# Chunked attention on one core: the off-diagonal weight blocks replaced by folded states

## Chip, core and metric

The kernel runs on one core of a Trainium2 chip, in one launch. The metric is the device time of that launch in microseconds (us). Everything is float32.

## What is computed

The input `x` has 8 sequences of 256 tokens with 256 features. One layer is computed: `x + attention(layernorm(x)) + ffn(layernorm(x))`. The change touches only the second half of the attention, for 16 heads with key and value size 128 and 64 memory slots (M = 64):

```
q, k = rope(hs @ Wq.T), rope(hs @ Wk.T);  v = hs @ Wv.T
s    = clip(hs @ Ws1.T @ Ws2.T + bs2);  es = exp(s);  enz = exp(-cumlogsumexp(s))
A    = causal(q @ k.T) * scale
ok   = enz * (A @ es)                 # T x M
qv   = softmax(ok)                    # T x M
W2   = causal((qv * enz) @ es.T)      # T x T
o    = W2 @ v                         # T x 128
out  = (rmsnorm(o) * silu(g)) @ Wo.T
```

A sequence of 256 tokens is two chunks of 128. In `W2` there are three blocks of 128 by 128 that aren't zero: two on the diagonal, which are triangular, and one below it, which is full: second chunk's queries against first chunk's keys.

## The kernel before

Tokens are taken in four groups of 512 (two sequences each, `TC` = 4 chunks of 128), heads in pairs. One step `n` is one group and one pair of heads, so there are 32 steps. A step's stages are functions: `rope` (q and k), `value` and `gate` (both through `vg`), `states` (es, es transposed, enz), `scores`, `logits`, `softmax`, `turn` (the softmax transposed and multiplied by enz: `prT`), `weights`, `outputs`, `turn_back`, and every second step `close` (the product with Wo). The feed-forward part (`ffn_block`, `ffn_down`) is fed in between these stages.

The order of the work is written out by hand. Each stage has a place in its step, a fraction in the table `POS` at the top of the file; the loop at the end of `layer_kernel` sorts the stages of a step by it and calls them. A stage issues its TensorE work at once and leaves the work of the other engines behind as a generator in `chains`; each call of `tick()` moves every such generator on by one piece. `need(...)` ticks until the given generators are through, and so only sets the order in which instructions are issued; the waits on the chip are semaphores. Step `n` runs the front of step `n` (scores, logits, softmax), the first stages of `n + 1` (states, rope) and the back of `n - 1` (turn, weights, outputs, turn_back).

All TensorE results go to PSUM tiles of one bank, taken from a pool of eight by `bank()`.

The stages that matter here, with the lines of their TensorE instructions in the kernel before:

- `states`: per chunk one product at L401 and one at L402, contraction 17, 128 output columns. The operands of L401 lie on partitions 0 to 16, those of L402 on 32 to 48, so that they use different row groups of the array.
- `logits`, L526: for both heads `j` of the pair, lhsT is 64 columns of `es`, and the result goes to partitions 0 to 63 or 64 to 127: two column groups.
- `weights(n, b)`, L596 and L600, called for both sequences `b` at places 0.179 and 0.209: contraction 64, the operands of head `j` on partitions 64j to 64j+63 (two row groups), results in one bank for each head. L596 gives the first diagonal block and the block below the diagonal at once (256 columns), L600 the second diagonal block (128 columns). `masked` (L497, VectorE) multiplies the 128 x 384 result by the mask into a tile `at`.
- `outputs(n, j)`, L617, L618 and L621: for each sequence three full 128 x 128 x 128 products, diagonal, below the diagonal, diagonal; the last two add up in PSUM. Then ScalarE squares and sums (L629), VectorE and GpSimd make the norm (L633, L634), and VectorE multiplies by it and by the gate into `og` (L638), reading the bank of the outputs.

Of the kernel before, what the change touches and what calls it, by code (L numbers as in the profile page):

```python
# [13 lines left out]
ALU = mybir.AluOpType  # L14
# [3 lines left out]
P = 128  # L18
B, T, D = 8, 256, 256
H, DK, M = 16, 128, 64  # L20
# [4 lines left out]
TC = G // P  # L25
# [8 lines left out]
 'turn': (0,),  # L34
 'logits': (0.144,),
 'softmax': (0.255,),
 'weights': (0.179, 0.209),
 'low': (0.176,),
 'states': (0.223,),
# [21 lines left out]
def layer_kernel(ctx: ExitStack, tc: tile.TileContext, a: dict, out: bass.AP):  # L61
# [30 lines left out]
    def need(*gens):  # L92

        while any(c in chains for c in gens):
            tick()
# [7 lines left out]
    def new(pool, shape, tag, bufs=1, dtype=F32):  # L103

        users = held.setdefault(tag, [])
        if len(users) >= bufs:
            need(*users[-bufs])
        t = pool.tile(shape, dtype, tag=tag, name=tag, bufs=bufs)
        users.append([])
        at_tag[id(t)] = t, users[-1]  # L110
        return t
# [3 lines left out]
    def chain(gen, *tiles):  # L115

        chains.append(gen)
        for t in tiles:
            at_tag[id(t)][1].append(gen)
        return gen  # L120

    def bank():
        return new(ps_p, [P, 512], "ps", 8)
# [60 lines left out]
    def norm(g, h):  # L184

        st = new(ln, [P, 2, 6], "st", 2)
        mv = new(ln, [P, 2, 2], "mv", 2)
        rstd = new(ln, [P, 2], "rstd", 2)
        xn = new(ln, [P, 2, D], "xn", 2)
        for i in range(2):  # L190
            nc.vector.bn_stats(st[:, i, :], res[:, g * TC + h + i, :])
            nc.vector.bn_aggr(mv[:, i, :], st[:, i, :])
        nc.vector.tensor_scalar(rstd, mv[:, :, 1], EPS, None, ALU.add)
        nc.gpsimd.tensor_tensor(rstd, rstd, nhalf[:, 0:2], ALU.pow)
        yield
        for i in range(2):
            nc.vector.tensor_scalar(
                xn[:, i, :], res[:, g * TC + h + i, :], mv[:, i, 0:1],
                rstd[:, i : i + 1], ALU.subtract, ALU.mult,
            )  # L200
        yield
        ps = bank()
        for c in range(2):
            for i in range(2):
                nc.tensor.transpose(
                    ps[:, (2 * c + i) * P : (2 * c + i + 1) * P], xn[:, i, c::2], ident
                )
        t = g * G + h * P

        def work():  # L210
            nc.scalar.copy(xT[:, :, t : t + 2 * P], ps.rearrange("p (c t) -> p c t", c=2))
            yield

        normed.setdefault(g, []).append(chain(work(), ps, xn))
        yield
# [174 lines left out]
    def states(n):  # L390

        g, hp = steps[n]
        ms = slice(hp * P, (hp + 1) * P)
        (rT, c), to = rTs[g], of[n]
        need(c)
        es = to["es"] = new(p1, [P, TC, P], "es")
        esT = to["esT"] = new(p2, [P, G], "esT", 2)
        ps, psT = bank(), bank()
        for i in range(TC):
            ts = slice(i * P, (i + 1) * P)  # L400
            nc.tensor.matmul(ps[:, ts], lhsT=rT[0:17, ts], rhs=w_s2[0:17, ms], start=True, stop=True)  # L401
            nc.tensor.matmul(  # L402
                psT[:, ts], lhsT=w_s2[32:49, ms], rhs=rT[32:49, ts], start=True, stop=True
            )


        enz = to["enz"] = new(p2, [P, G], "enz", 2)

        def work():
            both = ((esT, psT), (es.rearrange("p i m -> p (i m)"), ps))  # L410
            for t, q in both:
                nc.vector.tensor_scalar(t, q, CLAMP, -CLAMP, ALU.min, ALU.max)  # L412
            yield
            for t, q in both:
                nc.scalar.activation(t, t, AF.Exp)  # L415
            yield
            for b in range(2):
                e = esT[:, b * T : (b + 1) * T]

                nc.vector.tensor_tensor_scan(  # L420
                    enz[:, b * T : (b + 1) * T], e, e, 0.0, ALU.add, ALU.max
                )
            yield
            for i in range(TC):
                r = enz[:, i * P : (i + 1) * P]
                nc.vector.reciprocal(r, r)  # L426
                yield

        to["states"] = chain(work(), ps, psT, es, esT, enz)
# [65 lines left out]
    def masked(ts, pss):  # L495
        for t, ps in zip(ts, pss):
            nc.vector.tensor_tensor(t, ps[:, 0 : 3 * P], mask, ALU.mult)  # L497
        yield

    def scores(n, j):  # L500

        (q, qc), (k, kc) = of[n]["q", j], of[n]["k", j]
        need(qc, kc)
        pss, ats = [], []
        for b in range(2):
            ps = bank()
            nc.tensor.matmul(  # L507
                ps[:, 0:T], lhsT=k[:, b, 0:P], rhs=q[:, b, :], start=True, stop=True
            )
            nc.tensor.matmul(  # L510
                ps[:, T : T + P], lhsT=k[:, b, P:T], rhs=q[:, b, P:T], start=True, stop=True
            )
            pss.append(ps)
            ats.append(new(p2, [P, 3 * P], "at", 5))
        of[n]["at", j] = ats, chain(masked(ats, pss), *ats, *pss)

    def logits(n):
# [64 lines left out]

        to["turn"] = chain(work(), ps, prT, to["pr"], enz)

    def weights(n, b):

        to = of[n]
        need(to["turn"])
        prT, esT = to["prT"], to["esT"]
        pss, wt = [bank(), bank()], []  # L590
        t0 = b * T
        for j in range(2):
            wt.append(new(p2, [P, 3 * P], "at", 5))
        for j in range(2):
            mj = slice(j * M, (j + 1) * M)
            nc.tensor.matmul(  # L596
                pss[j][:, 0:T], lhsT=esT[mj, t0 : t0 + P], rhs=prT[mj, t0 : t0 + T],
                start=True, stop=True,
            )
            nc.tensor.matmul(  # L600
                pss[j][:, T : T + P], lhsT=esT[mj, t0 + P : t0 + T], rhs=prT[mj, t0 + P : t0 + T],
                start=True, stop=True,
            )
        to["wt", b] = wt, chain(masked(wt, pss), *wt, *pss)

    def outputs(n, j):

        to = of[n]
        need(to["wt", 0][1], to["wt", 1][1], *(to[k, i] for k in ("v", "sg") for i in (0, 2)))
        v, sg, eps = to["v"], to["sg"], to["eps"]  # L610
        pot = bank()
        po = pot.rearrange("p (i d) -> p i d", d=DK)
        for b in range(2):
            w = to["wt", b][0][j]
            v0 = v[:, 2 * b, j * DK : (j + 1) * DK]
            v1 = v[:, 2 * b + 1, j * DK : (j + 1) * DK]
            nc.tensor.matmul(po[:, 2 * b, :], lhsT=w[:, 0:P], rhs=v0, start=True, stop=True)  # L617
            nc.tensor.matmul(  # L618
                po[:, 2 * b + 1, :], lhsT=w[:, P : 2 * P], rhs=v0, start=True, stop=False
            )  # L620
            nc.tensor.matmul(  # L621
                po[:, 2 * b + 1, :], lhsT=w[:, 2 * P : 3 * P], rhs=v1, start=False, stop=True
            )
        ss = new(p2, [P, TC], "ss", 2)
        og = new(p2, [P, TC, DK], "og", 2)

        def work():
            for i in range(TC):
                nc.scalar.activation(  # L629
                    og[:, i, :], po[:, i, :], AF.Square, accum_out=ss[:, i : i + 1]  # L630
                )
            yield
            nc.vector.scalar_tensor_tensor(ss, ss, 1.0 / DK, eps[:, j::2], ALU.mult, ALU.add)  # L633
            nc.gpsimd.tensor_tensor(ss, ss, nhalf, ALU.pow)  # L634
            yield
            yield
            for i in range(TC):
                nc.vector.scalar_tensor_tensor(  # L638
                    og[:, i, :], po[:, i, :], ss[:, i : i + 1],
                    sg[:, i, j * DK : (j + 1) * DK], ALU.mult, ALU.mult,  # L640
                )

        to["og", j] = og, chain(work(), pot, ss, og, eps, sg)
# [40 lines left out]
    for n in range(-1, N + 1):  # L684
# [3 lines left out]
        def put(name, k, f, *args):  # L688
            place = pos.get(name, POS[name])
            at.append((place[k], len(at), f, args))  # L690
# [35 lines left out]
            put_norm(gn, NORM_AT)  # L726
        if n > 0:
            put("turn", 0, turn, n - 1)
            for k in range(2):
                put("weights", k, weights, n - 1, k)  # L730
                put("outputs", k, outputs, n - 1, k)
                put("back", k, turn_back, n - 1, k)
            if n % 2 == 1 and n > 1:
                for k in range(2):
                    put("close", k, close, n - 2, 2 * k)
            if n == N:
                for k in range(2):
                    put_at(2.0, close, N - 1, 2 * k)
# [81 lines left out]
```

## Time and profile before

| | |
|---|---|
| median of three runs | 1279.37 us (1279.18 to 1280.09) |
| the profiled execution | 1279.47 us, of which 1277.6 us are the span from its first to its last instruction |
| busy share of the span | TensorE 99%, VectorE 64%, ScalarE 42%, GpSimd 35% |
| granted TensorE clock | 1.000 |

The profile lists an instruction by its line and by the names of the tiles it writes and reads, with partitions x elements. Every float32 product appears as two matmul records (256 of L596 are 128 products, 4 in each of 32 steps). Records of TensorE overlap: one takes longer from start to end than the time until the next one starts, so what a record costs TensorE is read as the distance from its start to the next start.

### The profile page before, as it was taken

Reading aid. Unit: us, or ns where it says so; the run is one execution under the profiler, and the core shown is the slowest. Engines: PE = TensorE matmul, PEld = TensorE weight load, DVE = VectorE, ACT = ScalarE, POOL = GpSimd, SP = SyncE. Lnnn points to the kernel's source line nnn. Section 1 sums busy time; section 2 is a strip of 40 time slices with the busy share of each in tenths; the row PEclk is TensorE's granted clock in tenths of the full one; section 3 lists DMA queues with packets and bytes.
Section 4 is the critical chain, followed back from the end, with each engine's and each line's share of the span. In section 5 each row is a group of like instructions: output and inputs, shape, how many; then the busy total and the mean of one; then the engine's idle time right before and its main releaser. Section 6 shows DMA issues by size and latency. Waiting matters only on the chain.

```text
span 1277.6 us, 17557 instructions
## 1 busy us (share of the span) xinstructions
PE 1262.4 (99%) x6448; PEld 914.2 (72%) x6448; DVE 817.4 (64%) x1592; ACT 531.9 (42%) x1677; POOL 441.9 (35%) x408
## 2 busy tenths in 40 slices
PE   7999999999999999999999999999999999999998
PEld 4577777776777777767677687777777767777776
DVE  6968756666656576664665766756665566566444
ACT  2444443453433454352444424445343345434232
POOL 4434333443223443232433413444332344322311
PEclk9999999999999999999999999999999999999999
DMA  4301111110111110011110010101001111101000
GB/s 162 116 17 50 34 33 50 34 49 2 50 34 34 50 33 18 17 34 50 50 34 17 31 38 33 34 33 34 1 33 34 34 33 32 36 17 43 25 17 17
DMA packets 18361, 47.73 MB, mean 37 GB/s; under 512 B 1986, under 2 KB 6466, under 8 KB 18276
## 3 DMA queue, kind: packets, MB, share of 16 engines
q1 hardware_dynamic: 18276, 46.61, 11.1%
q8 instruction: 51, 0.84, 0.3%
q14 instruction: 34, 0.28, 0.1%
HBM read 44.51 MB, written 2.10 MB: 36 GB/s over the span
## 4 chain that ended last, share of the span: by engine, by line
PE 94%; DVE 4%; ACT 1%; issue 1%; POOL 0%; DMA 0%; POOLq 0%; DVEq 0%; ACTq 0%
PE ps L489 16%; PE ps L437 16%; PE ps L669 9%; PE ps L338 8%; PE ps L318 8%; PE ps L298 8%; PE ps L507 4%; PE ps L526 4%; PE ps L596 3%; PE ps L401 2%; PE ps L621 2%; PE ps L618 2%; PE ps L617 2%; PE ps L510 2%; PE ps L651 2%; PE ps L547 1%
## 5 line engine op out<-in xcount | busy, mean ns | idle before, releaser
L450 POOL TENSOR_TENSOR z<-z,sin 128x512 f32<-128x512 f32 x128 | 163.3, 1276 | 448.8 <-ACT z L447 448.5
L437 PE MATMUL ps<-xT,wts 128*128 128x512 f32 x512 | 240.9, 593 | 0.0
L489 PE MATMUL ps<-wts,xT 128*128 128x256 f32 x1024 | 239.7, 379 | 0.0
L489 PEld LDWEIGHTS ps<-wts,xT 128*128 128x128 f32 x1024 | 191.9, 190 | 55.8 <-issue 30.8
L437 PEld LDWEIGHTS ps<-xT,wts 128*128 128x128 f32 x512 | 94.3, 191 | 85.1 <-issue 79.3
L497 DVE TENSOR_TENSOR at<-ps,mask 128x384 f32<-128x384 f32 x256 | 129.2, 551 | 21.6 <-PE ps L510 9.4
L306 POOL TENSOR_SCALAR t<-t 128x512 f32<-128x512 f32 x64 | 40.1, 627 | 267.0 <-ACT t L304 265.0
L446 ACT COPY z<-ps 64x512 f32<-64x512 f32 x128 | 74.6, 583 | 135.9 <-PE ps L437 117.5
L415 ACT ACTIVATE esT<-esT 128x512 f32<-128x512 f32 x32 | 20.2, 630 | 252.4 <-DVE esT L412 252.4
L298 PE MATMUL ps<-xT,w_gate 128*128 128x512 f32 x256 | 120.7, 594 | 0.0
L318 PE MATMUL ps<-xT,w_up 128*128 128x512 f32 x256 | 120.6, 593 | 0.0
L277 DVE TENSOR_TENSOR res<-ps,res 128x512 f32<-128x512 f32 x64 | 44.1, 689 | 119.5 <-PE ps L338 59.8
L338 PE MATMUL ps<-w_down,inter 128*128 128x256 f32 x512 | 116.0, 380 | 0.9 <-DVE inter L326 0.9
L426 DVE RECIPROCAL enz<-enz 128x128 f32<-128x128 f32 x128 | 116.8, 932 | 0.0
L669 PE MATMUL ps<-w_o,ogT 128*128 128x256 f32 x512 | 115.6, 379 | 0.0
L338 PEld LDWEIGHTS ps<-w_down,inter 128*128 128x128 f32 x512 | 95.9, 190 | 14.4 <-DVE inter L326 1.7
L669 PEld LDWEIGHTS ps<-w_o,ogT 128*128 128x128 f32 x512 | 95.6, 190 | 14.6 <-issue 2.2
L448 DVE TENSOR_TENSOR k<-ps,cos 128x512 f32<-128x512 f32 x64 | 44.0, 687 | 87.2 <-ACT z L447 87.1
L451 POOL TENSOR_TENSOR q<-q,z 128x512 f32<-128x512 f32 x64 | 81.6, 1275 | 21.7 <-DVE q L448 13.9
L451 POOL TENSOR_TENSOR k<-k,z 128x512 f32<-128x512 f32 x64 | 81.5, 1273 | 9.0 <-DVE k L448 4.3
L448 DVE TENSOR_TENSOR q<-ps,cos 128x512 f32<-128x512 f32 x64 | 44.0, 688 | 63.0 <-ACT z L447 62.7
L559 ACT ACTIVATE pr<-ps,mx 128x64 f32<-128x64 f32 x256 | 76.5, 325 | 12.9 <-DVE mx L556 12.3
(81 smaller groups left out, 2119.5 us busy)
## 6 DMA issues: line engine op xcount, KB each, us to landing
wts<-in_wqkvg_dram SPq DMA_DIRECT2D x64, 512.0 KB, 3.6
pk<-in_codes_dram SPq DMA_DIRECT2D x12, 256.0 KB, 4.5
sc<-in_scales_dram SPq DMA_DIRECT2D x12, 256.0 KB, 4.7
w_o<-in_wo_dram SPq DMA_DIRECT2D x4, 512.0 KB, 6.0
out_dram<-res SPq DMA_DIRECT2D x8, 256.0 KB, 2.1
res<-in_x_dram SPq DMA_DIRECT2D x3, 512.0 KB, 5.4
res<-in_x_dram SPq DMA_DIRECT2D x2, 256.0 KB, 2.8
w_s<-in_ws_dram SPq DMA_DIRECT2D x3, 64.0 KB, 2.4
```

Of the source, the lines that this page charges most:

```text
L298: nc.tensor.matmul(pg, lhsT=w_gate[:, c, ns], rhs=xT[:, c, gs], start=c == 0, stop=c == 1)
L318: nc.tensor.matmul(pu, lhsT=w_up[:, c, ns], rhs=xT[:, c, gs], start=c == 0, stop=c == 1)
L338: nc.tensor.matmul(ps[:, k, :], lhsT=inter[g, n][0][:, (i + k) * P : (i + k + 1) * P], rhs=w_dn[:, n, :], start=n == 2 * q, stop=n == 2 * ...
L426: nc.vector.reciprocal(r, r)
L437: nc.tensor.matmul(ps, lhsT=w[:, c, :], rhs=xT[:, c, g * G : (g + 1) * G], start=c == 0, stop=c == 1)
L448: nc.vector.tensor_tensor(y, pv, cos_b, ALU.mult)
L450: nc.gpsimd.tensor_tensor(z, z, sin_b, ALU.mult)
L451: nc.gpsimd.tensor_tensor(y, y, z, ALU.add)
L489: nc.tensor.matmul(ps[:, k, :], lhsT=xT[:, c, tt], rhs=w[:, which, c, :], start=c == 0, stop=c == 1,)
L497: nc.vector.tensor_tensor(t, ps[:, 0 : 3 * P], mask, ALU.mult)
L559: nc.scalar.activation(pr[:, k, :], pv[:, k, :], AF.Exp, bias=mx[:, k : k + 1], scale=SCALE, accum_out=sm[:, k : k + 1],)
L669: nc.tensor.matmul(ps[:, k, :], lhsT=ogT[hh][0][:, (i + k) * P : (i + k + 1) * P], rhs=w_o[:, (hp // 2) * 4 + hh, :], start=hh == 0, stop= ...
```

## The change

Instead of forming the block of `W2` below the diagonal and multiplying it with the first chunk's values, the kernel multiplies the first chunk's `es` with its values once (a 64 x 128 state for each head and sequence) and multiplies the second chunk's `prT` with that state. The product is the same by associativity, since the block is full and needs no mask.

- A new stage `cross` (place 0.143, just ahead of `logits` at 0.144) issues four products for each step: lhsT is 64 columns of `es`, rhs 128 columns of `v`, results in two column groups of one bank. ScalarE copies the 128 x 256 result to a tile `cross`.
- `weights` is called once, at 0.179, for both sequences. It issues eight products of 128 columns, only the diagonal blocks, in two row groups, and VectorE masks 128 x 512 for each head into `wt`.
- A new stage `apply` (place 0.209) takes the two banks of the outputs and issues four products of 128 columns with contraction 64, in two row groups: `prT` of the second chunks with the state.
- `outputs` issues four products for each head and step (one for each chunk) in place of six, adding to what `apply` has left in the bank.
- `es` becomes double-buffered, since `cross` reads it a step later; `at` goes from five buffers to four; `xn` of `norm` shares the two buffers of rope's `z`.

```diff
+ 'cross': (0.143,),
...
-        xn = new(ln, [P, 2, D], "xn", 2)
+        xn = new(p2, [P, 2, D], "z", 2)
...
-        es = to["es"] = new(p1, [P, TC, P], "es")
+        es = to["es"] = new(p2, [P, TC, P], "es", 2)
...
-            ats.append(new(p2, [P, 3 * P], "at", 5))
+            ats.append(new(p2, [P, 3 * P], "at", 4))
...
+    def cross(n):
+        to = of[n]
+        need(*(to["v", i] for i in (0, 2)))
+        es, v = to["es"], to["v"]
+        ps = bank()
+        for b in range(2):
+            for j in range(2):
+                nc.tensor.matmul(
+                    ps[j * M : (j + 1) * M, b * DK : (b + 1) * DK],
+                    lhsT=es[:, 2 * b, j * M : (j + 1) * M],
+                    rhs=v[:, 2 * b, j * DK : (j + 1) * DK], start=True, stop=True,
+                )
+        z = new(p1, [P, 2 * DK], "cross")
+        def work():
+            nc.scalar.copy(z, ps[:, 0 : 2 * DK])
+            yield
+        to["cross"] = z, chain(work(), ps, z)
...
+    def weights(n):
...
+        for i in range(TC):
+            ts = slice(i * P, (i + 1) * P)
+            for j in range(2):
+                mj = slice(j * M, (j + 1) * M)
+                nc.tensor.matmul(
+                    pss[j][:, ts], lhsT=esT[mj, ts], rhs=prT[mj, ts], start=True, stop=True
+                )
+        tri_b = tri.unsqueeze(1).to_broadcast([P, TC, P])
         for j in range(2):
+            wt = new(p2, [P, TC, P], "wt", 2)
+            def work(wt=wt, ps=pss[j]):
+                nc.vector.tensor_tensor(
+                    wt, ps.rearrange("p (i q) -> p i q", q=P), tri_b, ALU.mult
+                )
+                yield
+            to["wt", j] = wt, chain(work(), wt, pss[j])
...
+    def apply(n):
+        to = of[n]
+        z, c = to["cross"]
+        need(c)
+        prT = to["prT"]
+        to["po"] = [bank(), bank()]
+        for b in range(2):
+            for j in range(2):
+                mj = slice(j * M, (j + 1) * M)
+                nc.tensor.matmul(
+                    to["po"][j][:, (2 * b + 1) * P : (2 * b + 2) * P],
+                    lhsT=prT[mj, (2 * b + 1) * P : (2 * b + 2) * P],
+                    rhs=z[mj, b * DK : (b + 1) * DK], start=b == 0, stop=False,
+                )
     def outputs(n, j):
...
+        for i in range(TC):
             nc.tensor.matmul(
+                po[:, i, :], lhsT=wt[:, i, :], rhs=v[:, i, j * DK : (j + 1) * DK],
+                start=False, stop=i == TC - 1,
             )
...
             put("turn", 0, turn, n - 1)
+            put("cross", 0, cross, n - 1)
+            put("weights", 0, weights, n - 1)
+            put("weights", 1, apply, n - 1)
             for k in range(2):
-                put("weights", k, weights, n - 1, k)
```

More of the change, by code (lines that the diff above doesn't have):

```diff
@@ L583, in turn @@
         to["turn"] = chain(work(), ps, prT, to["pr"], enz)
-    def weights(n, b):
+    def cross(n):
[16 more added lines that the diff above has]
+    def weights(n):
         to = of[n]
@@ L589, in weights @@
         prT, esT = to["prT"], to["esT"]
-        pss, wt = [bank(), bank()], []
-        t0 = b * T
-        for j in range(2):
[L593 to L603, printed above, removed]
@@ L604, in weights @@
-        to["wt", b] = wt, chain(masked(wt, pss), *wt, *pss)
+        pss = [bank(), bank()]
+        for i in range(TC):
[6 more added lines that the diff above has]
+        tri_b = tri.unsqueeze(1).to_broadcast([P, TC, P])
+        for j in range(2):
+            wt = new(p2, [P, TC, P], "wt", 2)
[5 more added lines that the diff above has]
+            to["wt", j] = wt, chain(work(), wt, pss[j])
@@ L606, in outputs @@
     def outputs(n, j):
         to = of[n]
-        need(to["wt", 0][1], to["wt", 1][1], *(to[k, i] for k in ("v", "sg") for i in (0, 2)))
+        wt, c = to["wt", j]
+        need(c, *(to["sg", i] for i in (0, 2)))
         v, sg, eps = to["v"], to["sg"], to["eps"]
-        pot = bank()
+        pot = to["po"][j]
         po = pot.rearrange("p (i d) -> p i d", d=DK)
[L613 to L617, printed above, removed]
+        for i in range(TC):
@@ L618, in outputs @@
             nc.tensor.matmul(
[L619 to L622, printed above, removed]
+                po[:, i, :], lhsT=wt[:, i, :], rhs=v[:, i, j * DK : (j + 1) * DK],
+                start=False, stop=i == TC - 1,
             )
```

## The prediction

> **What bounds the kernel.** I read the shares of busy time first, then the chain that ended last, then the waits of TensorE alone, and last the timeline of the two stages that change. From the page, the line of engine shares and the chain by engine:
>
> ```profile
> PE 1262.4 (99%) x6448; PEld 914.2 (72%) x6448; DVE 817.4 (64%) x1592; ACT 531.9 (42%) x1677; POOL 441.9 (35%) x408
> ...
> PE 94%; DVE 4%; ACT 1%; issue 1%; POOL 0%; DMA 0%; POOLq 0%; DVEq 0%; ACTq 0%
> ```
>
> TensorE is busy for 99% and is 94% of the chain. A busy TensorE need not be bound by its own work, so I ask for its waits (us in total, times, longest):
>
> ```profile
> PE ps L205 <- DVE xn L197: 8.3, 3, 6.5
> PE ps L526 <- DVE at L497: 1.5, 1, 1.5
> PE ps L338 <- DVE inter L326: 0.9, 2, 0.5
> PE ps L379 <- ACT xT L211: 0.7, 1, 0.7
> ```
>
> These are all: 11.4 us of 1277.6, most of it at the start. In the steady steps TensorE never waits. So the time is the sum of what TensorE's records cost it, from start to start, and other engines count only where they begin to make it wait.
>
> The timeline of TensorE shows those costs. First the weights of one step, followed by its states (start, duration, line, count):
>
> ```profile
> 600.60 0.71 PE L596 MATMUL ps<-prT,esT 64*128 64x256 f32 x4
> 601.14 0.40 PE L600 MATMUL ps<-prT,esT 64*128 64x128 f32 x4
> 601.36 0.70 PE L596 MATMUL ps<-prT,esT 64*128 64x256 f32 x4
> 601.79 0.49 PE L600 MATMUL ps<-prT,esT 64*128 64x128 f32 x4
> 602.21 0.37 PE L401 MATMUL ps<-w_s,rT 17*128 17x128 f32 x1
> 602.22 0.37 PE L402 MATMUL ps<-rT,w_s 17*128 17x128 f32 x1
> 602.42 0.27 PE L401 MATMUL ps<-w_s,rT 17*128 17x128 f32 x1
> 602.43 0.27 PE L402 MATMUL ps<-rT,w_s 17*128 17x128 f32 x1
> 602.54 0.27 PE L401 MATMUL ps<-w_s,rT 17*128 17x128 f32 x1
> 602.54 0.27 PE L402 MATMUL ps<-rT,w_s 17*128 17x128 f32 x1
> ...
> 603.30 0.33 PE L547 MATMUL ps<-ident,ok 128*128 128x128 f32 x1
> ```
>
> L401 and L402, in different row groups, start within 0.01 us of each other, and the next pair follows 0.11 us later: two row groups cost what one costs. All eight states products (eight pairs of records) take 602.21 to 603.30, 1.09 us. The eight weights products take 600.60 to 602.21, 1.61 us. Now the outputs:
>
> ```profile
> 610.68 0.38 PE L617 MATMUL ps<-v,at 128*128 128x128 f32 x2
> 610.90 0.39 PE L618 MATMUL ps<-v,at 128*128 128x128 f32 x2
> 611.13 0.39 PE L621 MATMUL ps<-v,at 128*128 128x128 f32 x2
> ...
> 613.36 0.59 PE L437 MATMUL ps<-xT,wts 128*128 128x512 f32 x1
> ```
>
> Twelve full products, 610.68 to 613.36: 2.68 us, 0.223 each (0.112 a record). They use the whole array, and nothing pairs.
>
> [...] states cost 1.09 us where eight pairs at 0.109 make 0.87, so 0.22 goes at entry and exit; for the weights it is 0.31 (below). [...] L401 and L402 both count as busy in the same 1.09 us. So I sum distances between starts.
>
> **The change, part by part**, for one step, then times 32. A record of 128 columns costs 0.109 us (pairs of L401/L402 follow at 0.105 to 0.112), one of 256 columns 0.2155 (records of L669 start 0.216 apart).
>
> 1. `outputs`: 12 full products become 8. 4 x 0.223 = **-0.89 us**. That they add to a bank that `apply` began costs nothing that the trace knows of: L621 does it after L618 at the same 0.22.
>
> 2. `weights`: each row group had 4 records of 256 and 4 of 128 columns, 4 x 0.2155 + 4 x 0.109 = 1.30 us; measured 1.61, so 0.31 is entry, exit and a slip between the groups. Now each group has 8 records of 128: 0.87. With the same 0.31 it is 1.18 us: **-0.43 us**. Ends for the 0.31: 0.22, as for the states, and 0.42, if one more slip of a record comes in.
>
> 3. `apply`: 4 records in each row group, 4 x 0.109 = **+0.44 us**. In the built order it follows the weights directly, in the same mode, and `states` follows it as it did the weights, so there is no further change of mode. Unpaired it would be 0.87; nothing lets it be below 0.42 (0.105 a record).
>
> 4. `cross`: 4 records in each column group, **+0.44 us**. In the built order it stands directly before `logits`, which is in the same mode (L526, 128 x 64), so again no change of mode. Bounds as for `apply`.
>
> 5. VectorE: four masks of 128 x 384 at 0.55 us become two of 128 x 512; the nearest row, 128 x 512 from PSUM (L448), is 0.69. That is 2.20 to 1.38 us. VectorE has 36% idle and TensorE doesn't wait for it: nothing, and at best the 1.5 us that L526 waited for `at` in the whole run.
>
> 6. ScalarE: one more copy of 128 x 256. The row of the copy of v, 128 x 512, is the upper end:
>
> ```profile
> L463 ACT COPY v<-ps 128x512 f32<-128x512 f32 x64 | 37.3, 585 | 23.2 <-PE ps L489 22.7
> ```
>
> At most 0.59 x 32 = 19 us of ScalarE, beside 58% idle. It adds a wait: `apply` waits for this copy, and behind `apply` TensorE's whole queue. Between the end of `cross` and `apply` lie logits (1.45 us from the first L526 to the first L596 in an ordinary step) and weights (1.18): 2.6 us, against 0.6 for the copy and some tenths for the two handovers. What may stand before it in ScalarE's queue is a Square or Tanh of the feed-forward. In the built order all of those have their TensorE source done at least 0.6 us before `cross` ends, and the late Tanhs of the trace (which end 1.9 to 3.5 us into logits in seven steps) come behind the copy. Cost 0; upper end 3 us in all. Queued behind the copy is the Exp of `states`, whose inputs come later anyway.
>
> 7. Masks to outputs: before, the first two masks could run while the second sequence's weights did; now both wait for all of them. From the end of the weights to the first outputs were 3.2 to 8.4 us, and `apply` adds 0.44. Masks and ok product need 2 x 0.69 + 0.69 = 2.1. Cost 0.
>
> 8. Banks: a step takes five (cross 1, weights 2, `apply` 2) where it took six (weights 4, outputs 2), but the two of the outputs are now held from `apply` until `og` is written. In the built order, the last two steps apart, the first TensorE instruction that waits for `og` comes 11.2 us of TensorE work after the outputs, as before the change. In the trace `og` is done 3.8 to 8.6 us after the last output record, but for 10.7 and 11.0 in the second step. Cost 0.
>
> 9. `xn` in the buffers of `z`: VectorE's L197 now waits for GpSimd's rope of k in steps 0, 2 and 5. In the first case GpSimd was done at 56.0 us and L197 began at 58.9. Cost 0, upper end 2 us. `es` doubled and `at` less one take nothing and wait for nothing: scores use four `at` a step, and weights use none now. The queues of SP and GpSimd keep all their instructions and DMAs in the same order.
>
> Sum: -0.89 - 0.43 + 0.44 + 0.44 = -0.45 us; unrounded (0.893 + 0.427 - 0.872) x 32 = **-14.3 us**. From the profiled execution's 1279.47 us that gives 1265.2; it stands 0.1 above the median of the runs.
>
> **Rivals.** *The new products don't pair.* Then `cross` and `apply` cost 0.87 each, +27.9 us in all: 1293 us, slower. The place is the records of the two new stages; it turns from faster to slower where a pair costs 0.165 us in place of 0.109 (14.3 us over 256 pairs). For it speaks only that no row shows 64 x 128 with contraction 64 in a long row of pairs; against it that L526, L596 and L401 pair in all three tilings used. *The outputs' banks come free too late.* Where `og` takes over 11.6 us, the wait is over 0.45 us a step and eats the gain; at 13 us it would be 1.8 x 32 = 58 us: 1323. For it speaks the chain of five hand-overs behind the outputs and that two of eight banks are held longer; against it 5 us of room in nearly every step. *The gain is eaten by waits and modes*: `apply` waits for its copy and splits the run, a second entry of 0.2 to 0.3 us, 6 to 10 us in all: 1271 to 1275. Against it stands the 2 us of room of part 6. *The change isn't what it says*: the built order has the counts 8, 4, 4, 8 in each step, so no chance is given to it.
>
> **The numbers.** The forecast (pairs as seen, no new wait) gets 0.82: 1265.2, with the bounds of parts 2 to 9, 1261 to 1270. Waits and modes 0.08, of which 0.02 lie within 0.2% (2.6 us, about what a measurement of this kernel can tell from no change). Unpaired 0.06, banks 0.04. Faster 0.88, within 0.2% 0.02, slower 0.10. The range 1261 to 1273 leaves out the two slower cases and the far end of the third.
>
> **What would show it.** In the profile after: `outputs` 8 products at 0.22, 1.78 us; `cross` and logits together about 1.9 us; weights and `apply` 1.6 us together, pairs 0.11 apart; no wait of TensorE on the `cross` copy, on `wt` or on `og`; TensorE's records up from 6448 to 6704, with its share still 99%. I am wrong if the waits of TensorE pass 15 us in total, or if records of the new lines start one after the other, not two by two.

## The result, and the profile after

The changed kernel takes 1268.34 us (median of 4 runs, 1267.43 to 1268.65) against 1279.73 before in the same session; the ratio is 0.9911, with a 95% interval of 0.9899 to 0.9923. Forecast were 1265.2 us, with a range of 1261 to 1273. The direction and the range held; 3 us of the gain are missing. The profiled execution took 1268.5 us, of which 1266.5 are its span.

The page of the changed kernel, engine shares and chain by engine:

```profile
PE 1247.2 (98%) x6704; PEld 897.2 (71%) x6704; DVE 795.7 (63%) x1528; ACT 543.0 (43%) x1709; POOL 441.4 (35%) x408
...
PE 92%; DVE 5%; POOL 1%; issue 1%; ACT 1%; DMA 0%; POOLq 0%; DVEq 0%; ACTq 0%
```

The record count is the 6704 that was counted beforehand. But TensorE went from 99% to 98% and from 94% to 92% of the chain, and GpSimd, which had 0%, has 1%. All waits of TensorE in the changed kernel (total, times, longest):

```profile
PE ps L206 <- DVE z L198: 12.3, 4, 7.1
PE ps L527 <- DVE at L498: 1.5, 1, 1.5
PE ps L380 <- ACT xT L212: 0.7, 1, 0.7
PE ps L339 <- DVE inter L327: 0.7, 2, 0.5
```

No line names `cross`, `wt` or `og`. The one that grew is the first: the transposes of the layer norm wait for `z`, the buffer that was `xn` before; 8.3 us in three waits became 12.3 in four. Now an ordinary step, timeline of TensorE in the changed kernel, from `cross` to the outputs:

```profile
633.72 0.66 PE L595 MATMUL ps<-v,es 128*64 128x128 f32 x8
634.21 1.47 PE L527 MATMUL ps<-at,es 128*64 128x256 f32 x16
635.61 1.16 PE L618 MATMUL ps<-prT,esT 64*128 64x128 f32 x16
636.60 0.61 PE L644 MATMUL ps<-cross,prT 64*128 64x128 f32 x8
637.15 0.37 PE L402 MATMUL ps<-w_s,rT 17*128 17x128 f32 x1
...
640.45 1.05 PE L659 MATMUL ps<-v,wt 128*128 128x128 f32 x8
641.34 1.88 PE L299 MATMUL ps<-xT,w_gate 128*128 128x512 f32 x4
643.06 1.05 PE L659 MATMUL ps<-v,wt 128*128 128x128 f32 x8
643.95 1.88 PE L438 MATMUL ps<-xT,wts 128*128 128x512 f32 x4
```

From start to start: `cross` and logits 1.89 us (forecast 1.9), weights and `apply` 635.61 to 637.15, 1.54 us (forecast 1.62), outputs 0.89 + 0.89 = 1.78 us (forecast 1.78). The steps are as forecast or better, and so they are all through the run: weights and `apply` take 1.54 us in each of the 32. So what is missing isn't in them. It is at 130 us, in step 2, where the norm of the third token group runs. Timeline of the changed kernel there:

```profile
129.46 1.27 POOL L451 TENSOR_TENSOR z<-z,sin 128x512 f32<-128x512 f32 x1 [0.25 <-ACT z L448]
130.81 1.26 POOL L452 TENSOR_TENSOR k<-k,z 128x512 f32<-128x512 f32 x1
132.11 1.91 DVE L198 TENSOR_SCALAR z<-res,mv,rstd 128x256 f32<-128x256 f32 x2 [2.07 <-POOL k L452]
133.46 0.36 PE L206 MATMUL ps<-ident,z 128*128 128x128 f32 x1 [3.35 <-DVE z L198]
```

GpSimd finishes rope's k at 132.07; VectorE, which stood idle for 2.07 us, then writes the normalised tokens into the buffer that k's rope has just left; TensorE has stood idle for 3.35 us when it can transpose them. In the kernel before, the same VectorE instruction (L197) had a buffer of its own. It began 3.2 us before GpSimd finished rope's k (L451), and TensorE came to the transposes (L205) without a gap:

```profile
129.03 2.00 DVE L197 TENSOR_SCALAR xn<-res,mv,rstd 128x256 f32<-128x256 f32 x2
130.63 0.27 PE L205 MATMUL ps<-ident,xn 128*128 128x128 f32 x1
130.96 1.28 POOL L451 TENSOR_TENSOR k<-k,z 128x512 f32<-128x512 f32 x1
```

The stretches around the place in the changed kernel show a second loss. The columns are from:to and length in us, busy time of TensorE, its weight loads, VectorE, ScalarE and GpSimd (with the number of instructions), granted TensorE clock, DMA share, GB/s:

```profile
130.00:133.40 3.40, 0.11 (x1) 0.00 (x0) 1.33 (x3) 2.38 (x5) 3.24 (x4) 1.00 0.82 272
133.40:137.00 3.60, 3.28 (x13) 2.94 (x14) 3.60 (x6) 1.15 (x2) 0.47 (x1) 0.55 0.03 9
137.00:141.00 4.00, 4.00 (x19) 2.86 (x19) 2.73 (x7) 0.07 (x1) 0.00 (x0) 0.98 0.00 0
```

TensorE is busy for 0.11 of 3.40 us in the first, and in the next its granted clock is 0.55: behind the 3.35 us of idle time it is 0.50 from 133.7 to 137.1 us, for 3.4 us. In a run below (weights_by_head) the half clock followed 2.83 us of idle time. From the first L299 of this place to the first L319 behind it (128.23 to 138.99 us) TensorE takes 10.76 us. The same records, L298 to L318, took 5.69 us in the kernel before (128.91 to 134.60). That is 5.1 us lost: 3.5 ahead of the first transpose and 1.6 from there on, at half clock.

### The profile page after: what moved, and what is told of

Its sections match the earlier page's. It is cut to its first block, busy times and chain, and to the rows that moved or that the text cites. A ratio compares the mean times of both kernels' runs of the same rounds, so it can differ in the third digit from the quotient of the medians.

```text
span 1266.5 us, 17998 instructions
## 1 busy us (share of the span) xinstructions
PE 1247.2 (98%) x6704; PEld 897.2 (71%) x6704; DVE 795.7 (63%) x1528; ACT 543.0 (43%) x1709; POOL 441.4 (35%) x408
## 4 chain that ended last, share of the span: by engine, by line
PE 92%; DVE 5%; POOL 1%; issue 1%; ACT 1%; DMA 0%; POOLq 0%; DVEq 0%; ACTq 0%
PE ps L490 16%; PE ps L438 16%; PE ps L708 9%; PE ps L339 9%; PE ps L319 8%; PE ps L299 8%; PE ps L659 4%; PE ps L508 4%; PE ps L527 3%; PE ps L618 3%; PE ps L402 2%; PE ps L511 2%; PE ps L690 2%; PE ps L595 1%; PE ps L548 1%; PE ps L577 1%
## 5 line engine op out<-in xcount | busy, mean ns | idle before, releaser
L451 POOL TENSOR_TENSOR z<-z,sin 128x512 f32<-128x512 f32 x128 | 163.3, 1275 | 435.5 <-ACT z L448 434.8
L299 PE MATMUL ps<-xT,w_gate 128*128 128x512 f32 x256 | 120.8, 594 | 0.0
L319 PE MATMUL ps<-xT,w_up 128*128 128x512 f32 x256 | 120.6, 593 | 0.0
L708 PEld LDWEIGHTS ps<-w_o,ogT 128*128 128x128 f32 x512 | 95.6, 190 | 14.6 <-issue 2.2
L659 PEld LDWEIGHTS ps<-v,wt 128*128 128x128 f32 x512 | 65.0, 192 | 20.5 <-issue 19.8
L677 DVE SCALAR_TENSOR_TENSOR og<-ps,ss,sgate 128x128 f32<-128x128 f32 x256 | 70.0, 339 | 14.7 <-POOL ss L673 14.3
L673 POOL TENSOR_TENSOR ss<-ss,nhalf 128x4 f32<-128x4 f32 x64 | 64.8, 1017 | 39.8 <-DVE ss L672 38.1
```

Source lines behind the costliest of these rows:

```text
L299: nc.tensor.matmul(pg, lhsT=w_gate[:, c, ns], rhs=xT[:, c, gs], start=c == 0, stop=c == 1)
L319: nc.tensor.matmul(pu, lhsT=w_up[:, c, ns], rhs=xT[:, c, gs], start=c == 0, stop=c == 1)
L451: nc.gpsimd.tensor_tensor(z, z, sin_b, ALU.mult)
L659: nc.tensor.matmul(po[:, i, :], lhsT=wt[:, i, :], rhs=v[:, i, j * DK : (j + 1) * DK], start=False, stop=i == TC - 1,)
L708: nc.tensor.matmul(ps[:, k, :], lhsT=ogT[hh][0][:, (i + k) * P : (i + k + 1) * P], rhs=w_o[:, (hp // 2) * 4 + hh, :], start=hh == 0, stop= ...
```

## The experiments

Theory 1: the missing time is the shared buffer of `xn` and `z`, in one place. Theory 2: it is spread over the steps, in the new stages. Times are medians; the kernel before stood at 1279.6 to 1279.9 us in each comparison.

**xn_own: the change without the sharing.**

```diff
-        xn = new(p2, [P, 2, D], "z", 2)
+        xn = new(ln, [P, 2, D], "xn", 2)
...
-        u = new(de, [P, 2, CH], "u", 2, I32)
+        u = new(de, [P, 2, CH], "u", 1, I32)
...
-        z = new(p1, [P, 2 * DK], "cross")
+        zt = new(p1, [P, TC * 2, M], "pr")
+        z = zt.rearrange("p k m -> p (k m)")[:, 0 : 2 * DK]
...
-        to["cross"] = z, chain(work(), ps, z)
+        to["cross"] = z, chain(work(), ps, zt)
```

> The changed kernel with xn in two buffers of its own again; to make room, the decoder's u has one buffer (VectorE alone uses it) and the cross state lies in the tile of pr, which is free then. Theory 1 (the missing 3 us of the gain are the shared z buffers in step 2: a stall of TensorE of 3.5 us and half a clock for 3.4 us after it, 5.6 us against 0.6 before): about 5 us faster than the changed kernel, 1263.3 us, and no wait of TensorE on xn over 2 us at 130 us. Theory 2 (the missing time is spread over the steps, in the new stages): no change, 1268.3 us.

Measured: 1263.11 us, ratio to the kernel before 0.9869 (0.9852 to 0.9885). The wait is back to what it was, and the clock drops nowhere but in the last 2 us (mean granted clock 0.999). Waits of TensorE, first line:

```profile
PE ps L206 <- DVE xn L198: 8.6, 3, 6.5
```

That is 5.2 us better than the changed kernel, as theory 1 has it. This version beats both kernels.

**before_xn_in_z: the sharing without the rest.**

```diff
-        xn = new(ln, [P, 2, D], "xn", 2)
+        xn = new(p2, [P, 2, D], "z", 2)
```

> The kernel before with one part of the change alone: xn shares the two buffers of rope's z. Theory 1: VectorE waits in step 2 until GpSimd has finished the rope of k (about 132.2 us), the transposes of xn come about 3 us later than before, the clock drops after it: slower by 4 to 5 us, 1284 us. Theory 2: no change, 1279.7 us.

Measured: 1285.12 us, ratio 1.0041 (1.0026 to 1.0056), slower by 5.2 us. The same stall stands in its timeline:

```profile
133.22 1.91 DVE L197 TENSOR_SCALAR z<-res,mv,rstd 128x256 f32<-128x256 f32 x2 [2.07 <-POOL k L451]
...
134.58 0.42 PE L205 MATMUL ps<-ident,z 128*128 128x128 f32 x1 [3.05 <-DVE z L197]
```

Taken away or put in alone, the sharing is worth 5.2 us. Theory 1 is shown, theory 2 has fallen.

**scale_early: GpSimd's load in that step.**

```diff
-                put_at(0.3 + 0.04 * h, scale_wo, h)
+                put_at(0.01 * h, scale_wo, h)
```

> The changed kernel, with the four scalings of w_o on GpSimd (1.12 us each) moved from the places 0.30 to 0.78 of step 2 to its first eighth. Theory 1: GpSimd reaches the rope of k in step 2 at least 1.1 us earlier, so the stall falls from 3.5 to about 2.3 us, and with it perhaps the half clock: 1 to 3 us faster than the changed kernel, 1265 to 1267 us. If only the shared buffer counts and not GpSimd's load: no change, 1268.3 us. Theory 2: no change.

Measured: 1264.64 us, 3.7 us faster than the changed kernel, more than expected. TensorE lost 0.8 us at the transposes and 0.6 just ahead of them in place of 3.5, and the half clock didn't come there. So the four scalings of w_o, 1.12 us each between the ropes, and the clock make up most of the cost, but not the wait itself: VectorE still waits 1.49 us for the rope of k. In step 5 of the changed kernel, where GpSimd has no such extra load, VectorE waits as long as in step 2:

```profile
249.78 0.74 DVE L198 TENSOR_SCALAR z<-res,mv,rstd 128x256 f32<-128x256 f32 x2 [2.07 <-POOL k L452]
...
253.28 0.63 PE L206 MATMUL ps<-ident,z 128*128 128x128 f32 x4
```

There TensorE loses nothing, since it comes to the transposes 2.8 us after VectorE is through. What a wait of VectorE costs depends on how soon TensorE needs the result.

**no_cross: the price of the two new stages.** Both `put` lines of `cross` and `apply` are taken out, and `outputs` takes its own bank. The kernel then leaves out what the second chunks' queries get from the first chunks' keys.

> The changed kernel without the stages cross and apply; its output leaves out what the second chunks' queries get from the first chunks' keys. It measures what the two stages cost in all. Pairs as in L401 and L402, 0.109 us each, and no change of mode: 0.87 us a step, 27.9 us in all, so 1240.4 us. Unpaired: 1268.3 - 55.8 = 1212.5 us. If cross or apply also brings waits or an entry of 0.2 us a step: 1234 us.

Measured: 1240.21 us in one run, 28.1 us below the changed kernel, where 27.9 were expected for pairs without any further wait or change of mode (of tiling). From start to start its trace lacks 13.8 us at `cross` and logits and 14.4 us at weights and `apply`.

**cross_twice_one and cross_twice_both: do the groups pair?** The products of `cross` are issued once more, for head 0 alone or for both heads.

```diff
+        for b in range(2):
+            for j in range(1):        # range(2) in the sister
+                nc.tensor.matmul(
+                    ps[j * M : (j + 1) * M, b * DK : (b + 1) * DK],
+                    lhsT=es[:, 2 * b, j * M : (j + 1) * M],
+                    rhs=v[:, 2 * b, j * DK : (j + 1) * DK], start=True, stop=True,
+                )
```

> The changed kernel with the two products of cross for head 0 issued a second time (one column group only): four more records of 128 columns a step in that group. Theory A (two groups side by side cost what one costs): 4 x 0.109 x 32 = 14 us, 1282.3 us. Theory B (the array does one record at a time): the same 14 us. It is the measure for its sister, in which both heads are doubled.

> The changed kernel with all four products of cross issued a second time: eight more records a step, four in each column group. Theory A (groups side by side): again 14 us, 1282.3 us, as with one head doubled. Theory B (one record at a time): 28 us, 1296.2 us.

Measured: 1282.95 and 1282.76 us, 14.6 and 14.4 above the changed kernel. Twice as many added products cost the same, so the second column group is free beside the first. The rival "unpaired" has fallen. In both traces `cross` and logits take 2.32 us a step in place of 1.89, which makes 13.8 us. Most of the rest lies at the place at 130 us, where the half clock lasted 6.8 us in these two profiles and not 3.4 (mean granted clock 0.997 in both, 0.999 in the changed kernel).

**cross_apart: a run of its own.**

```diff
- 'cross': (0.143,),
+ 'cross': (0.09,),
```

> The changed kernel with cross at place 0.09, between the scores of the two heads, where it stands alone among full-array products and not before logits, which has the same tiling. Theory A (each change of tiling costs TensorE 0.15 to 0.3 us, as at the entry of logits and of states): 5 to 10 us slower, 1273 to 1278 us. Theory B (the change of tiling is hidden or the cost beside the pairs lies in something else): no change, 1268.3 us.

Measured: 1278.66 us, 10.3 us slower than the changed kernel, 0.32 a step: nearly the whole gain. In its trace the four products stand between the scores of the two heads. They take 0.59 us, 0.15 more than their four pairs at 0.109, and the full products just ahead and just behind lose 0.1 each. That `cross` stands beside logits is what makes the change worth its while.

**weights_by_head: the order in which row groups are issued.**

```diff
-        for i in range(TC):
-            ts = slice(i * P, (i + 1) * P)
-            for j in range(2):
-                mj = slice(j * M, (j + 1) * M)
+        for j in range(2):
+            mj = slice(j * M, (j + 1) * M)
+            for i in range(TC):
+                ts = slice(i * P, (i + 1) * P)
```

> The changed kernel with the eight products of weights issued head by head (all of row group 0, then all of row group 64) and not in turn. In the kernel before, L596 and L600 were issued head by head, and its weights lost 0.31 us a step beside the pairs; the changed kernel, in turn, loses 0.23. Theory A (the order of issue makes the groups slip by one record): 0.08 to 0.11 us a step back, 2.6 to 3.5 us slower than the changed kernel, 1271 to 1272 us. Theory B (the slip came from the second call's waits in the kernel before, not from the order): no change, 1268.3 us. If the groups only run side by side when issued in turn: 8 x 0.109 x 32 = 28 us slower, 1296 us.

Measured: 1286.01 us, 17.7 us slower than the changed kernel: none of the three times that were expected. Timeline of TensorE:

```profile
606.93 1.37 PE L618 MATMUL ps<-prT,esT 64*128 64x128 f32 x13
608.04 0.37 PE L644 MATMUL ps<-cross,prT 64*128 64x128 f32 x1
608.15 0.27 PE L618 MATMUL ps<-prT,esT 64*128 64x128 f32 x1
608.26 0.27 PE L644 MATMUL ps<-cross,prT 64*128 64x128 f32 x1
608.26 0.27 PE L618 MATMUL ps<-prT,esT 64*128 64x128 f32 x1
...
609.02 0.37 PE L402 MATMUL ps<-w_s,rT 17*128 17x128 f32 x1
```

Weights and `apply` take 2.09 us, not 1.54. The first record of row group 64 started 0.55 us after the first of group 0, when that had five records under way or done, and it stayed five behind: `apply` (L644) is at work in group 0 while the last L618 of group 64 are still to come. 0.55 x 32 = 17.6 us.

**before_in_turn and weights_by_two: how far one group falls behind.** The first issues L596 for both heads and then L600 for both, in the kernel before; the second issues two products of head 0, two of head 1, and again, in the changed kernel.

```diff
             nc.tensor.matmul(
                 pss[j][:, 0:T], lhsT=esT[mj, t0 : t0 + P], rhs=prT[mj, t0 : t0 + T],
                 start=True, stop=True,
             )
+        for j in range(2):
+            mj = slice(j * M, (j + 1) * M)
             nc.tensor.matmul(
```

```diff
-            for j in range(2):
+        for k in range(TC * 2):
+            i, j = k // 4 * 2 + k % 2, k // 2 % 2
```

> The kernel before, with the four products of each call of weights issued in turn: L596 of head 0, L596 of head 1, then the two of L600. Theory A ([...] products issued head by head leave the second group behind): the slip of one record goes, 0.08 to 0.11 us a step, 2.6 to 3.5 us faster than the kernel before, 1276.3 to 1277.2 us, and the loss beside the pairs falls from 0.31 to 0.23 us. Theory B (the slip comes from the waits of the second call): no change, 1279.8 us.

> The changed kernel with weights issued by two: two products of head 0, two of head 1, and again. With four in a row for each head the second group stayed five records behind, 0.55 us a step. Theory A [...]: with two in a row the second group stays one record behind or none, as in the kernel before: 0 to 0.11 us a step, 1268.3 to 1271.8 us. If any order other than strictly in turn serialises the groups: half of the loss of four in a row or more, 8 us, 1276 us.

Measured: 1276.27 us, ratio 0.9973 (0.9963 to 0.9984), 3.3 us faster than the kernel before; the loss beside the pairs fell from 0.31 to 0.21 us a step. And 1271.07 us, 2.7 us slower than the changed kernel, with 0.33 in place of 0.23. Two products of a head in a row left the other group one record behind (0.10 us a step), four left it five behind (0.55 us). What sets these distances isn't shown. The slip in the kernel before came from its order of issue, and what the changed kernel won beyond the sum in this term, 2.6 us (0.081 x 32), came from issuing in turn.

**seven_banks: is the bank pool at its limit?**

```diff
-        return new(ps_p, [P, 512], "ps", 8)
+        return new(ps_p, [P, 512], "ps", 7)
```

The pool itself gets seven banks too.

> The changed kernel with seven PSUM banks in its pool in place of eight. The rival that the outputs' banks come free too late, or that the pool is at its limit since two banks are held from apply on: slower by over 0.45 us a step, 1283 us or more. My theory (5 us of room at the outputs' banks, nearly every bank free long before it is asked for): 1268 to 1271 us.

Measured: 1269.11 us (two runs), 0.8 us above the changed kernel. The difference hides two things that work against each other. TensorE has new waits: three for `og` and `wt` of 1.1, 0.4 and 0.4 us, and three of 0.3 us for other tiles. The longest is

```profile
PE ps L438 <- DVE og L677: 1.1, 1, 1.1
```

With them, TensorE comes later to the place at 130 us. It stands idle there for 1.42 us in place of 3.35, and the half clock doesn't come (mean granted clock 1.000): record by record, 2.8 us less are lost there. Taking a bank away thus costs some 3.6 us (an estimate: 0.8 and 2.8), a quarter of the 14 us at which this rival begins. It has fallen.

## Why the prediction was right in direction, and where it missed

- **What bounds the kernel**: right. TensorE is 94% and 92% of the chain, and the sum of its start-to-start distances gave the gain of the steps. But by one of its own signs the forecast was wrong: the waits of TensorE, 15.2 us as listed above, pass 15 in total, and its share is 98% and not still 99%. Both come from part 9.
- **Parts 1, 3 and 4** (`outputs`, `apply`, `cross`): right to about a hundredth of a us a step in the timeline; the two stages cost 28.1 us for a forecast 27.9.
- **Part 2** (`weights`): the term for entry, exit and slip was sized 0.31 us and is 0.23, since the new loop issues the heads in turn. It is 0.01 above the lower end given. Gain 2.6 us more than the sum had.
- **Parts 5 to 8** (masks, copy, outputs, banks): right at cost 0; no wait of TensorE names them. Part 7 read 3.2 to 8.4 us from the weights to the outputs; the last step has only 1.8, less than the 2.1 that it wanted, and no wait came of that either.
- **Part 9** failed. It put the shared buffer of `xn` and `z` at "Cost 0, upper end 2 us", and it cost 5.1 in the traces (5.2 in both experiments). It looked at the first of the three norms only, where GpSimd was through 2.9 us before VectorE asked, and took that for all. In step 2 the scalings of w_o load GpSimd, and the k that VectorE then waits for was finished at 132.24 us in the kernel before, 3.2 us after L197 had begun: the trace of before had the number. That step is also the one in which TensorE comes to the transposes at once. And the half clock after a long idle time, 1.6 us, wasn't thought of.
- **The sum**: -14.3 forecast, -2.6 from the order of issue, +5.1 from the buffer make -11.8; the spans differ by 11.1. Of the rest, 0.6 us lie at the very start, where the first transpose came at 7.1 and not 6.5 us. VectorE's first instruction (L192) waited until 4.06 us for the load of `x` in this profile, until 3.46 in the one before (L191). The change has no part in it: weights_by_head, with the same norm and the shared buffers, has 3.49 us. That the forecast lies 3 us from the measured time is in part luck, since the two errors have opposite signs; without the shared buffer the time is 1263.1 us (xn_own).
- **The rivals**: unpaired and banks have fallen by experiment. "Waits and modes" put 6 to 10 us on a wait for the copy and a second change of mode. Neither came. cross_apart shows what a change of mode would have cost, had `cross` not stood where it does: 10.3 us.

## What to carry to other kernels

When TensorE bounds a kernel, add up the distances between the starts of its records, and treat products in different row or column groups as one, provided that they are issued in turn and stand beside work in the same tiling: here a pair cost the 0.109 us of one record, four products of a head in a row cost 0.55 us a step, and a short run in a tiling of its own 0.32. When a change frees memory by letting two tiles share a buffer, look up each place where the one must wait for the other's last reader, above all where that reader's engine has extra work and where the bounding engine needs the result at once. A long stall of TensorE can cost more after it has ended, by the clock: here 3.5 us were followed by 1.6 more, at a granted clock of 0.50.

## What the runs showed of the hardware

- Records of two groups started almost together: 6 to 7 ns apart for L401 and L402 and 13 to 14 for the two heads of L596 in the kernel before, 6 to 7 for L618 and L644 in the changed kernel, where the next pair followed after 0.105 us in most cases.
- Row groups ran out of program order against each other: in weights_by_head a record of `apply` in group 0 started at 608.04 us, while earlier instructions of group 64 started up to 608.37. But they did so at a price: with two products of one group issued in a row, the other group fell one record behind (0.10 us a step), with four in a row, five records (0.55 us), and it didn't catch up in the same run (weights_by_two, before_in_turn, weights_by_head).
- A record in a second column group cost nothing: eight more records or four more, 14.4 and 14.6 us over the run.
- At the same place of the program, idle times of 3.35 us (after), 3.05 (before_xn_in_z) and 2.83 (weights_by_head) were followed by half clock; 1.42 us (seven_banks), and 0.45 and 0.62 close to each other (scale_early), were not. The half clock lasted 3.4 us in the first two (mean granted clock of the execution 0.999 and 0.998) and 6.8 in weights_by_head, cross_twice_one and cross_twice_both (0.997). The length of the idle time alone doesn't tell: at the start of the changed kernel TensorE had no work for 7.08 us, and the clock behind it, from 7 to 20 us, was 1.00.
- Four products in another tiling between full ones took 0.15 us more than their pairs, and the full products on either side lost 0.1 each (cross_apart).
